# Node sums with features on partitions, node inputs made a group ahead, lead of 22

## The chip, the cores and the metric

The kernel runs on one NeuronCore of one Trainium2 chip. The metric is device time in microseconds (us). TensorE (PE), VectorE (DVE), ScalarE (ACT) and GpSimd (POOL) each work through their own queue of instructions in order; SyncE (SP) issues DMAs. An instruction waits on semaphores for those on other engines, and what stands behind it on its engine waits with it.

## The reference

One layer of a graph network with a normalisation ahead and a residual behind, N = 6250 nodes of D = 256 features, E = 206250 edges sorted by target node (33 a node on average), all in f32:

```python
h   = maximum(layernorm(x), 0)
e   = relu(raw @ W_e1.T + b_e1) @ W_e2.T + b_e2        # raw: 64 features an edge
emb = (e * (clip(polarity, 0, 1) + 0.01)) @ W_le.T + b_le
msg = relu(h[src] + emb)
agg = segment_sum(msg, dst, num_segments=N)
t   = (h + agg) @ W_g1.T + b_g1
out = x + relu(layernorm(t) * ln_g + ln_b) @ W_g2.T + b_g2
```

## The kernel before

**Start.** `nodes_out` computes h in chunks of 512 nodes, adds b_le and stores the sum as hb_d in DRAM (DVE's statistics, ACT's normalisation L324, POOL's addition L328, SP's store L329). The row statistics, 1/std and -mean/std of each node, remain in rs_s and nm_s, nodes on partitions. W_e2 and W_le are multiplied into one matrix wc_s, their biases into bc_s. Meanwhile the first LEAD = 20 units of edges go through their dense part.

**Edges.** A unit is 256 edges, two units make a block of 512, two blocks a pair, for which SP loads the raw features (L210, 256 KB, four buffers). There are 806 units. For each unit `edge_part` runs eight matmuls' records of L241 into PSUM (pz) and DVE adds bc_s (L246) into msg; on some of the first units ACT copies (L244) and DVE adds later (L502). Every fourth unit is a turn: the first layer of the pair after next (L223 on PE, L227 on ACT), then the sums that have become possible, then the next load. PSUM has seven buffers pz, shared by all of this.

POOL gathers the rows hb_d[src] by indirect DMA into hg (16 buffers, two gathers a unit). When they are there, `whole` computes relu(msg * polarity + hg): two DVE operations (L504) and one of ACT (L506). It follows `edge_part` at a distance of LEAD units, which falls by one every 36 units down to one.

**Sums.** A group is six blocks, 3072 edges of consecutive targets, in four strands of 32 rows each. `select` makes one-hot matrices (L494), and `add_up` adds the messages of a block into pd in PSUM (L514). After the last block of a group ACT copies pd to ms (L520): 128 rows of partial node sums.

**Nodes.** A window is 128 nodes (49 windows). Its sum comes from the two or three groups that may hold its edges: those within MARGIN = 1024 edges of the expected place, 146 pairs in all. When the last of them is done, `node_work` puts steps on a list by unit number; after each unit `due` runs one of those that have come due. The steps and their distance in units:

- `spread` (1 unit after the group's end): SP loads x (L183), DVE makes a one-hot matrix s for each group (L556);
- `rows_of` (2 later): PE multiplies the one-hots with ms (L565, the nodes on the partitions of the result), ACT computes h of the window from x (L567), DVE adds both into a (L568);
- `turned` (2 later): PE transposes a (L141), ACT copies the result to aT (L144);
- `one` (2 later): PE multiplies by W_g1 (L153), DVE adds the bias and normalises (L155 to L159);
- `two` (3 later): PE transposes (L165), ACT applies scale, offset and relu (L168);
- `three` (2 later): PE multiplies by W_g2 (L175), DVE adds bias and x (L177, L178), SP stores (L179).

The order of instructions on every engine is the order in which this program emits them. The function any_order, behind a condition at the end, is for edges in another order and isn't run with this input.

Of the kernel before, what the change touches and what calls it, by code (L numbers as in the profile page):

```python
# [12 lines left out]
ALU = mybir.AluOpType  # L13
# [24 lines left out]
MARGIN = 1024  # L38
DEG = E // N
LEAD = 20  # L40
# [4 lines left out]
CH = 4  # L45
assert DEG * N == E and NF * GE + S * P >= E
# [32 lines left out]

def rows(ap, t, p, n):  # L80
    return ap[t * P:t * P + p * n, :].rearrange("(t p) d -> p t d", p=p)
# [3 lines left out]
def gnn_kernel(ctx: ExitStack, tc: tile.TileContext, x, src_c, dst_c, dst_r, pol_c, raw_t, w_e1t, w_e2,  # L85
               w_let, w_g1t, w_g2t, vec_c, row_v, out):
# [4 lines left out]
    hb_d = dram.tile([N, D], F32, name="hb_d")  # L91

# [41 lines left out]
    def finish_nodes(nd, ps, w, n):  # L134
# [37 lines left out]
        def third(nT, xt):  # L172
# [6 lines left out]
            nc.sync.dma_start(out=out[bass.ds(r, n), :], in_=ot[:n])  # L179

        def load_x():
            xt = nd.tile([P, D], F32, name="xt3")
            nc.sync.dma_start(out=xt[:n], in_=x[bass.ds(r, n), :])  # L183
            return xt
# [6 lines left out]
    with fast:  # L191
# [20 lines left out]
        def first_layer(q):  # L212
# [12 lines left out]
            for c in range(2):  # L225
                for s, b in enumerate(bs):
                    nc.scalar.activation(e1[b][:, c, :], pe[s, c], AF.Relu, bias=be1_s[:, c:c + 1])  # L227
            raw.pop(q)

        def plain(u):  # L230

            return u < LEAD and u % 2 == 1
# [33 lines left out]
        nc.vector.memset(ones, 1.0)  # L266
        make_identity(nc, ident)
# [24 lines left out]
        with tc.tile_pool(name="p1", bufs=4) as p1, tc.tile_pool(name="p1x", bufs=6) as p1x:  # L292
# [4 lines left out]
            def load_rows(k, halves=1):  # L297
                if k < len(parts):
# [3 lines left out]
                    for i in range(halves):  # L302
                        nc.sync.dma_start(out=xts[k][:p, i * h:(i + 1) * h], in_=rows(x, t0 + i * h, p, h))
# [12 lines left out]
            def nodes_out(k):  # L316
# [12 lines left out]
                nc.sync.dma_start(out=rows(hb_d, t0, p, t), in_=hb[:p, :t])  # L329
# [30 lines left out]
            load_rows(4)  # L360
            load_pair(3)
            first_layer(0)
            lists = {3: (src_s, src_c), 5: (pol_s, pol_c), 7: (dst_f.bitcast(I32), dst_c)}
            for k in range(len(parts) + 1):
# [6 lines left out]
                if k:  # L371
                    nodes_out(k - 1)
                    load_rows(k + 4)
                    u = next(units, None)
                    if u is not None:
                        forward(u)
# [6 lines left out]
                if k % 2:  # L383
# [6 lines left out]
                if k == len(parts) - 3:  # L390
                    nc.vector.tensor_scalar(pol_s, pol_s, 0.0, 1.0, op0=ALU.max, op1=ALU.min)
                    nc.vector.tensor_scalar_add(pol_s, pol_s, 0.01)
            for u in units:
                forward(u)

# [16 lines left out]
        def rows_of_edges():  # L412
# [4 lines left out]
            nc.vector.tensor_tensor(rel[:, full:], dst_f[:, full:], base_b[:, NF, :], ALU.subtract)  # L417

# [42 lines left out]
        with tc.tile_pool(name="hg", bufs=HG) as hg_p, tc.tile_pool(name="ms", bufs=5) as ms_p, \  # L461
                tc.tile_pool(name="sel2", bufs=9) as sel2_p, tc.tile_pool(name="nd", bufs=2) as nd, tc.tile_pool(name="idx", bufs=HG) as idx_p:
# [45 lines left out]
            def add_up(b):  # L508
# [9 lines left out]
                if b == blocks_of(g)[-1]:  # L518
# [26 lines left out]
            def node_work(w, spread_now=False):  # L545
                n = min(P, N - w * P)
                gs = groups_of(w)
                box = {}
                turn, first, second, third, load_x = finish_nodes(nd, ps, w, n)

                def spread():
                    box["xt"] = load_x()
                    box["sel2"] = []
# [5 lines left out]
                    if not spread_now:  # L559
                        at(now + 2, rows_of)  # L560

                def rows_of():
                    pa = ps()
                    for i, g in enumerate(gs):
                        nc.tensor.matmul(pa[:n, 0, :], box["sel2"][i][:, :n], ms[g], start=i == 0, stop=i == len(gs) - 1)  # L565
# [233 lines left out]
```

## Time and profile before

| what | value |
|---|---|
| median of 10 runs | 2664.91 us (2655.61 to 2673.22) |
| the profiled execution | 2669.87 us, its span 2668.1 us |
| mean granted TensorE clock in it | 0.949 |
| PE busy in 0 to 20 us, and in the 28 us from 2640 on | 13.71 and 16.40 us |
| PE busy in 400 to 600 and 1400 to 1600 us | 183.42 and 173.84 us |
| first gather | 76.54 us |

The span runs from the first to the last instruction; the profiled execution's own time contains it. A group's line in the profile names line, engine, operation, tiles (out<-in) and count, then busy time and the mean duration of one in ns, and then the idle time of the engine just before these instructions and what ended it. A matmul in f32 appears as two records; records overlap, so the mean duration of one is longer than its share. The granted clock is the share of TensorE's full clock that was granted.

### The profile page before, as it was taken

The page shows a single profiled execution, that of the slowest core. Times are in us where ns is not written, and L with a number is a line of the kernel's source. Part 1 is how long each engine was busy: PE and PEld are TensorE (multiplying, and loading weights), DVE is VectorE, ACT ScalarE, POOL GpSimd, SP SyncE. Part 2 cuts the span into 40 slices and gives each one's busy share as a digit, 9 for nine tenths or more (in the row PEclk, how much of TensorE's full clock was granted, in tenths as well). Part 3 has the DMA queues.
Part 4 walks back from the last instruction along what each step waited for, and adds up shares of the span by engine and source line. Part 5 has one row for each costly group of instructions (what it writes and reads, how often), then busy time and mean ns, then how long its engine had stood idle before and what let it go on. Part 6 is the DMA issues. An engine that isn't in the chain of part 4 may idle for free.

```text
span 2668.1 us, 35462 instructions
## 1 busy us (share of the span) xinstructions
PE 2376.5 (89%) x12188; PEld 1643.3 (62%) x12188; DVE 1483.6 (56%) x3982; ACT 1115.7 (42%) x2003; POOL 1669.5 (63%) x1674
## 2 busy tenths in 40 slices
PE   8688989898999989899887988898899898988998
PEld 6456666566666656666665666665566666656665
DVE  5456555555565646555555565564466555556555
ACT  7234434344444434444433443443344443434343
POOL 5656656666666666666666666666666666666663
PEclk9889999999999989999998999999999999999999
DMA  7433333333333333333333333333334333333331
GB/s 268 122 103 107 105 115 109 103 114 113 104 115 102 114 109 114 109 100 113 113 107 99 109 110 110 100 110 101 114 105 118 106 101 112 110 103 106 110 108 54
DMA packets 135546, 296.34 MB, mean 111 GB/s; under 512 B 31256, under 2 KB 57408, under 8 KB 135360
## 3 DMA queue, kind: packets, MB, share of 16 engines
q0 software_dynamic: 77376, 211.39, 27.5%
q1 hardware_dynamic: 56848, 79.36, 9.4%
q10 hardware_dynamic: 1136, 3.27, 0.3%
q8 instruction: 97, 1.59, 0.3%
q14 instruction: 89, 0.73, 0.1%
HBM read 281.09 MB, written 12.80 MB: 110 GB/s over the span
## 4 chain that ended last, share of the span: by engine, by line
PE 78%; DVE 7%; issue 5%; another core or an unknown queue 5%; ACT 2%; DMA 1%; POOL 0%; SPq 0%; DVEq 0%; ACTq 0%; POOLq 0%
PE pz L241 48%; PE pz L223 13%; PE pd L514 8%; DVE hg L504 3%; PE pz L565 3%; PE pz L175 2%; PE pz L153 2%; DVE msg L246 2%; ACT hg L506 1%; PE pz L141 1%; DVE idx L474 1%; PE pz L165 0%; ACT aT L144 0%; DMA hg<-hb_d,idx 0%
## 5 line engine op out<-in xcount | busy, mean ns | idle before, releaser
L485 POOL DMA_INDIRECT hg<-hb_d,idx x1612 | 1633.0, 1013 | 934.4 <-DVE hg L504 431.9
L241 PE MATMUL pz<-wc_s,e 128*128 128x256 f32 x6448 | 1547.8, 393 | 45.5 <-issue 36.5
L241 PEld LDWEIGHTS pz<-wc_s,e 128*128 128x128 f32 x6448 | 1243.9, 196 | 307.4 <-issue 109.7
L246 DVE TENSOR_TENSOR msg<-pz,bc_s 128x512 f32<-128x512 f32 x796 | 545.8, 686 | 847.6 <-PE pz L241 345.7
L506 ACT ACTIVATE hg<-hg 128x512 f32<-128x512 f32 x806 | 507.4, 632 | 1204.3 <-DVE hg L504 1082.6
L504 DVE SCALAR_TENSOR_TENSOR hg<-msg,pol_s,hg 128x256 f32<-128x256 f32 x1612 | 703.0, 477 | 12.2 <-DMA hg<-hb_d,idx 11.7
L227 ACT ACTIVATE e<-pz,vecs 128x512 f32<-128x512 f32 x806 | 492.5, 685 | 168.9 <-PE pz L223 63.5
L223 PE MATMUL pz<-raw,we_s 64*128 64x512 f32 x1612 | 418.7, 621 | 18.2 <-DVE msg L246 8.2
L514 PE MATMUL pd<-hg,sel 128*32 128x256 f32 x3224 | 256.3, 390 | 56.1 <-issue 43.2
L223 PEld LDWEIGHTS pz<-raw,we_s 64*128 64x128 f32 x1612 | 144.7, 188 | 193.6 <-issue 163.7
L514 PEld LDWEIGHTS pd<-hg,sel 128*32 128x32 f32 x3224 | 92.4, 109 | 271.3 <-issue 214.0
L565 PE MATMUL pz<-ms,s 128*128 128x256 f32 (+1 forms) x292 | 92.5, 464 | 101.0 <-DVE s L556 86.3
L474 DVE COPY idx<-src_s 128x2 int32<-128x2 int32 x806 | 150.8, 190 | 0.0
L565 PEld LDWEIGHTS pz<-ms,s 128*128 128x128 f32 (+1 forms) x292 | 61.9, 224 | 123.8 <-issue 105.5
L177 DVE TENSOR_TENSOR ot<-pz,rows_b 128x256 f32<-128x256 f32 (+1 forms) x49 | 20.8, 424 | 196.2 <-PE pz L241 142.5
L153 PE MATMUL pz<-wg_s,aT 128*128 128x256 f32 (+1 forms) x196 | 57.1, 417 | 54.7 <-ACT aT L144 54.7
L520 ACT ACTIVATE ms<-pd 128x256 f32<-128x256 f32 x68 | 26.4, 388 | 133.4 <-PE pz L241 85.3
L153 PEld LDWEIGHTS pz<-wg_s,aT 128*128 128x128 f32 (+1 forms) x196 | 35.5, 197 | 73.1 <-ACT aT L144 69.5
L494 DVE TENSOR_TENSOR sel<-iota_w,rel 128x768 f32<-128x768 f32 x68 | 63.9, 940 | 0.0
L568 DVE TENSOR_TENSOR a<-a,pz 128x256 f32<-128x256 f32 (+1 forms) x49 | 20.7, 421 | 73.2 <-ACT a L567 41.1
L175 PE MATMUL pz<-wg_s,nT 128*128 128x256 f32 (+1 forms) x196 | 59.9, 432 | 1.0 <-DVE idx L474 0.7
L328 POOL TENSOR_TENSOR hb<-xt,rows_b 128x256 f32<-128x256 f32 (+1 forms) x49 | 34.9, 746 | 32.9 <-ACT xt L324 19.9
(73 smaller groups left out, 448.3 us busy)
## 6 DMA issues: line engine op xcount, KB each, us to landing
raw<-in_raw_t_dram SPq DMA_DIRECT2D x202, 256.0 KB
hg<-hb_d,idx POOLq DMA_INDIRECT x1612
hb_d<-hb SPq DMA_DIRECT2D x12, 512.0 KB
xt<-in_x_dram SPq DMA_DIRECT2D x48, 128.0 KB
out_dram<-ot SPq DMA_DIRECT2D x48, 128.0 KB
xt<-in_x_dram SPq DMA_DIRECT2D x11, 512.0 KB
src_s<-in_src_c_dram ACTq DMA_DIRECT2D x1, 806.0 KB
pol_s<-in_pol_c_dram ACTq DMA_DIRECT2D x1, 806.0 KB
```

Of the source, the lines that this page charges most:

```text
L153: nc.tensor.matmul(ph[:n, 0, :], aT[:, c, :n], wg1_s[:, c, :], start=c == 0, stop=c == 1)
L175: nc.tensor.matmul(po[:n, 0, :], nT[:, c, :n], wg2_s[:, c, :], start=c == 0, stop=c == 1)
L223: nc.tensor.matmul(pe[s, c], we1_s[s * F:(s + 1) * F, c * P:(c + 1) * P], raw[q][s * F:(s + 1) * F, :], start=True, stop=True)
L227: nc.scalar.activation(e1[b][:, c, :], pe[s, c], AF.Relu, bias=be1_s[:, c:c + 1])
L241: nc.tensor.matmul(pz[:, i, :], e1[b][:, c, k:k + P], wc_s[:, c, :], start=c == 0, stop=c == 1)
L246: nc.vector.tensor_add(msg[u], pz, bc_s)
L474: nc.vector.tensor_copy(idx[asked], src_s[:, 2 * asked:2 * asked + 2])
L485: nc.gpsimd.indirect_dma_start(out=hg[u][:, i, :], out_offset=None, in_=hb_d, in_offset=bass.IndirectOffsetOnAxis(ap=idx[u][:, i:i + 1], a ...
L504: nc.vector.scalar_tensor_tensor(hg[u][:, i, :], m[:, i, :], pol_s[:, 2 * u + i:2 * u + i + 1], hg[u][:, i, :], op0=ALU.mult, op1=ALU.add)
L506: nc.scalar.activation(hg[u], hg[u], AF.Relu)
L514: nc.tensor.matmul(pd[j * W:(j + 1) * W, g % 2, :], sel[g][:, k * S + j, :], m[:, j % 2, :], start=k == 0, stop=b == blocks_of(g)[-1])
L565: nc.tensor.matmul(pa[:n, 0, :], box["sel2"][i][:, :n], ms[g], start=i == 0, stop=i == len(gs) - 1)
```

## The change

The parts that the steps below touch:

- `rows_of` swaps its operands. ms is now the stationary one, in two halves of 128 features, and the one-hot the moving one, so the sum of a window comes out with features on partitions (two tiles of 128 x 128). `turned` goes, and with it L141, L144, and L567, L568. One DVE operation on PSUM adds the sum to relu of hT.
- hT is x of the window with features on partitions, from x_t, a transposed copy of x that is one more input. It is normalised by `ready`: two DVE operations with 1/std and -mean/std of the 128 nodes along the free axis, the same on all partitions. Those come from st_d in DRAM, which `stats_out` writes once (rs_s and nm_s transposed), by a load that repeats them over the partitions.
- `node_work` starts at the end of the group before the window's last: loads and one-hots 2 units after it, `ready` 3 units later. The sums come 2 units after the end of the last group. Then `one` 3, `two` 5, `three` 4 units apart (2, 3, 2 for the last windows). The buffers of node tiles go from 2 to 3.
- MARGIN is 768: 140 pairs of group and window. LEAD is 22.
- At the start x is loaded up to ten chunks ahead (11 buffers, 6 before), every third of the lead's units instead of every second is copied by ACT, one first-layer activation in four of the first blocks runs on DVE, the units stand in another rhythm, and the two operations on polarity come after the lead. The tail of 106 rows is moved in two DMAs of 96 and 10 rows.

```diff
-MARGIN = 1024
+MARGIN = 768
-LEAD = 20
+LEAD = 22
+AHEAD = 10
...
+def spread_out(p):
+
+    m = p - p % 16
+    return [(a, b) for a, b in ((0, m), (m, p)) if a < b]
...
-                    nc.scalar.activation(e1[b][:, c, :], pe[s, c], AF.Relu, bias=be1_s[:, c:c + 1])
+                    if b < 2 * LEAD // 4 + 4 and s == c == 1:
+                        nc.vector.tensor_scalar(e1[b][:, c, :], pe[s, c], be1_s[:, c:c + 1], 0.0, op0=ALU.add,
+                                                op1=ALU.max)
+                    else:
+                        nc.scalar.activation(e1[b][:, c, :], pe[s, c], AF.Relu, bias=be1_s[:, c:c + 1])
...
-            return u < LEAD and u % 2 == 1
+            return u < LEAD and u % 3 == 1
...
-                    load_rows(k + 4)
-                    u = next(units, None)
-                    if u is not None:
-                        forward(u)
+                    load_rows(k - 1 + AHEAD)
...
-                if k % 2:
+                for _ in range((k > 0) + (k > 2 and k % 3 > 0)):
...
-                if k == len(parts) - 3:
-                    nc.vector.tensor_scalar(pol_s, pol_s, 0.0, 1.0, op0=ALU.max, op1=ALU.min)
-                    nc.vector.tensor_scalar_add(pol_s, pol_s, 0.01)
             for u in units:
                 forward(u)
+            nc.vector.tensor_scalar(pol_s, pol_s, 0.0, 1.0, op0=ALU.max, op1=ALU.min)
+            nc.vector.tensor_scalar_add(pol_s, pol_s, 0.01)
...
+        def stats_out():
+
+            pt = ps()
+            for i, t in enumerate((rs_s, nm_s)):
+                nc.tensor.transpose(pt[:NW, i, :P], t, ident)
+            st_s = w0.tile([NW, 2, P], F32, name="st_s")
+            nc.scalar.activation(st_s, pt[:NW, :, :P], AF.Copy)
+            nc.sync.dma_start(out=st_d, in_=st_s)
...
                     for w in range(NW):
                         if groups_of(w)[-1] == g:
-                            late.pop(w, lambda: node_work(w))()
+                            late.pop(w)()
+                        elif groups_of(w)[-1] == g + 1 < NG - 1:
+                            late[w] = node_work(w)
...
+                far_apart = (3, 5, 4) if gs[-1] < NG - 3 else (2, 3, 2)
...
                 def spread():
                     box["xt"] = load_x()
+                    box["hT"] = nd.tile([P, 2, P], F32, name="hT")
+                    nc.sync.dma_start(out=box["hT"][:, :, :n], in_=x_t[:, :, w * P:w * P + n])
+                    st = nd.tile([P, 2, P], F32, name="stb")
+                    nc.sync.dma_start(out=st, in_=st_d[w:w + 1].to_broadcast([P, 2, P]))
+                    box["st"] = st
...
                     if not spread_now:
-                        at(now + 2, rows_of)
+                        at(now + 3, ready)
+
+                def ready():
+
+                    hT, st = box["hT"], box["st"]
+                    for i, op in enumerate((ALU.mult, ALU.add)):
+                        nc.vector.tensor_tensor(hT[:, :, :n], hT[:, :, :n], st[:, i:i + 1, :n].to_broadcast([P, 2, n]), op)

                 def rows_of():
+
+                    if spread_now:
+                        ready()
+                    hT = box["hT"]
                     pa = ps()
-                    for i, g in enumerate(gs):
-                        nc.tensor.matmul(pa[:n, 0, :], box["sel2"][i][:, :n], ms[g], start=i == 0, stop=i == len(gs) - 1)
-                    a = nd.tile([P, D], F32, name="a")
-                    nc.scalar.activation(a[:n], box["xt"][:n], AF.Relu, bias=nm_s[:n, w:w + 1], scale=rs_s[:n, w:w + 1])
-                    nc.vector.tensor_add(a[:n], a[:n], pa[:n, 0, :])
-                    box["a"] = a
-                    at(now + 2, turned)
-
-                def turned():
-                    box["aT"] = turn(box["a"])
-                    at(now + 2, one)
+                    for c in range(2):
+                        for i, g in enumerate(gs):
+                            nc.tensor.matmul(pa[:, c, :n], ms[g][:, c * P:(c + 1) * P], box["sel2"][i][:, :n],
+                                             start=i == 0, stop=i == len(gs) - 1)
+                    nc.vector.scalar_tensor_tensor(hT[:, :, :n], hT[:, :, :n], 0.0, pa[:, :, :n], op0=ALU.max, op1=ALU.add)
+                    at(now + far_apart[0], one)

                 def one():
-                    box["hs"] = first(box["aT"])
-                    at(now + 3, two)
+                    box["hs"] = first(box["hT"])
+                    at(now + far_apart[1], two)

                 def two():
                     box["nT"] = second(box["hs"])
-                    at(now + 2, three)
+                    at(now + far_apart[2], three)
...
                 if spread_now:
                     spread()
                 else:
-                    at(now + 1, spread)
-                return lambda: at(now + 1, rows_of)
+                    at(now + 2, spread)
+                return lambda: at(now + 1 + (gs[-1] < NG - 1), rows_of)
...
+        "x_t": laid(np.asarray(x).T.reshape(2, P, N).transpose(1, 0, 2)),
```

More of the change, by code (lines that the diff above doesn't have):

```diff
@@ L85, in gnn_kernel @@
 def gnn_kernel(ctx: ExitStack, tc: tile.TileContext, x, src_c, dst_c, dst_r, pol_c, raw_t, w_e1t, w_e2,
-               w_let, w_g1t, w_g2t, vec_c, row_v, out):
+               w_let, w_g1t, w_g2t, vec_c, row_v, x_t, out):
     nc = tc.nc
@@ L91, in gnn_kernel @@
     hb_d = dram.tile([N, D], F32, name="hb_d")
+    st_d = dram.tile([NW, 2, P], F32, name="st_d")
     def load(name, shape, src, eng):
@@ L178, in third @@
             nc.vector.tensor_add(ot[:n], ot[:n], xt[:n])
-            nc.sync.dma_start(out=out[bass.ds(r, n), :], in_=ot[:n])
+            for a, b in spread_out(n):
+                nc.sync.dma_start(out=out[bass.ds(r + a, b - a), :], in_=ot[a:b])
         def load_x():
             xt = nd.tile([P, D], F32, name="xt3")
-            nc.sync.dma_start(out=xt[:n], in_=x[bass.ds(r, n), :])
+            for a, b in spread_out(n):
+                nc.sync.dma_start(out=xt[a:b], in_=x[bass.ds(r + a, b - a), :])
             return xt
@@ L266, in gnn_kernel @@
         nc.vector.memset(ones, 1.0)
+        nc.vector.memset(rs_s, 0.0)
+        nc.vector.memset(nm_s, 0.0)
         make_identity(nc, ident)
@@ L289, in gnn_kernel @@
         be2_b = w0.tile([P, 2, P], F32, name="be2_b")
-        with tc.tile_pool(name="p1", bufs=4) as p1, tc.tile_pool(name="p1x", bufs=6) as p1x:
+        with tc.tile_pool(name="p1", bufs=4) as p1, tc.tile_pool(name="p1x", bufs=11) as p1x:
             parts = list(chunks())
@@ L302, in load_rows @@
                     for i in range(halves):
-                        nc.sync.dma_start(out=xts[k][:p, i * h:(i + 1) * h], in_=rows(x, t0 + i * h, p, h))
+                        for a, b in spread_out(p):
+                            nc.sync.dma_start(out=xts[k][a:b, i * h:(i + 1) * h], in_=rows(x, t0 + i * h, p, h)[a:b])
             def stats(k, i0, i1):
@@ L328, in nodes_out @@
                     nc.gpsimd.tensor_add(hb[:p, i, :], xt[:p, i, :], ble_b[:p])
-                nc.sync.dma_start(out=rows(hb_d, t0, p, t), in_=hb[:p, :t])
+                for a, b in spread_out(p):
+                    nc.sync.dma_start(out=rows(hb_d, t0, p, t)[a:b], in_=hb[a:b, :t])
             def product():
@@ L360, in gnn_kernel @@
             load_rows(4)
+            load_rows(5)
             load_pair(3)
+            for k in range(6, AHEAD):
+                load_rows(k)
             first_layer(0)
@@ L461, in gnn_kernel @@
         with tc.tile_pool(name="hg", bufs=HG) as hg_p, tc.tile_pool(name="ms", bufs=5) as ms_p, \
-                tc.tile_pool(name="sel2", bufs=9) as sel2_p, tc.tile_pool(name="nd", bufs=2) as nd, tc.tile_pool(name="idx", bufs=HG) as idx_p:
+                tc.tile_pool(name="sel2", bufs=9) as sel2_p, tc.tile_pool(name="nd", bufs=3) as nd, tc.tile_pool(name="idx", bufs=HG) as idx_p:
             idx = {}
@@ L604, in gnn_kernel @@
             for i, fn in enumerate((first_rows, rows_of_edges, lambda: select(0), lambda: select(1), row_numbers,
-                                    node_weights)):
+                                    node_weights, stats_out)):
                 at(LEAD + i, fn)
```

## The prediction

> **What bounds the kernel now.** I read the page's busy shares and its slices first, then the groups with the idle time before them, the table of waits, and last the timeline around a node step, with the granted clock of that stretch.
>
> The page of the kernel before (its span and engine rows, two groups of matmuls of the node work, the matmul group of the edges; a group's last part is the idle time of the engine just before it and what ended it):
>
> ```profile
> span 2668.1 us, 35462 instructions
> PE 2376.5 (89%) x12188; PEld 1643.3 (62%) x12188; DVE 1483.6 (56%) x3982; ACT 1115.7 (42%) x2003; POOL 1669.5 (63%) x1674
> ...
> L241 PE MATMUL pz<-wc_s,e 128*128 128x256 f32 x6448 | 1547.8, 393 | 45.5 <-issue 36.5
> ...
> L565 PE MATMUL pz<-ms,s 128*128 128x256 f32 (+1 forms) x292 | 92.5, 464 | 101.0 <-DVE s L556 86.3
> ...
> L153 PE MATMUL pz<-wg_s,aT 128*128 128x256 f32 (+1 forms) x196 | 57.1, 417 | 54.7 <-ACT aT L144 54.7
> ```
>
> TensorE is busy for 2376.5 of 2668.1 us and no other engine passes 63%, so PE bounds the kernel, and only its own work, its idle time (291.6 us) and its clock can change the time. Two rows of node work hold more than half of that idle time: 101.0 us before L565 and 54.7 us before L153, together 155.7 us, although they are only 150 us of PE's busy time. L241, with ten times the busy time, waits 45.5 us. In the table of waits (waiting engine and line, what ended the wait, sum, times, longest):
>
> ```profile
> DVE msg L246 <- PE pz L241: 345.7, 156, 7.5
> PE pz L565 <- DVE s L556: 86.3, 27, 8.7
> ACT ms L520 <- PE pz L241: 85.3, 29, 5.5
> PE pz L153 <- ACT aT L144: 54.7, 37, 3.8
> ```
>
> VectorE runs behind PE: its msg addition waits 7.5 us at worst for the signal of a matmul. By matching each L246 with the last L241 of its unit I get a lag of about 2.2 us in the middle and about 6 to 8 us in one unit of twenty. The one-hot tiles (L556) stand in that same queue only two units (2 x 1.73 us of PE) ahead of the matmuls that need them, so they come late. A timeline row shows it (start, duration, engine, line; in brackets the idle time before):
>
> ```profile
> 339.10 0.67 DVE L556 TENSOR_SCALAR s<-iota_p,rowid 128x128 f32<-128x128 f32 x3
> ...
> 339.50 1.54 PEld L565 LDWEIGHTS pz<-ms,s 128*128 128x128 f32 x6 [3.04 <-issue]
> 339.53 2.24 PE L565 MATMUL pz<-ms,s 128*128 128x256 f32 x6 [2.67 <-DVE s L556]
> ...
> 341.56 2.92 PE L241 MATMUL pz<-wc_s,e 128*128 128x256 f32 x8
> ```
>
> PE stood still for 2.67 us, ms (L520) had been written 4.46 us earlier, and only the one-hots were missing. It also pays afterwards: six L565 records take 2.24 us and eight L241 take 2.92, where after a wait of 1.32 us, at 300.58, the same groups took 1.53 and 1.89. The granted clock was 0.66 in the 5 us after the long wait and 1.00 after the short one. One long wait therefore costs another 0.71 + 1.03 = 1.74 us.
>
> **The change part by part**, against the profiled execution's 2669.9 us (span 2668.1).
>
> *One-hots a group ahead.* All that L565 waited for was L556. Issued with the loads about 12 units earlier, it is no longer late. What is late next is ms: its copy on ScalarE ends 4.7 us on average after the group's last L514 matmuls (1.9 us in the quickest tenth, 6.9 in the slowest). Against that, the order of instructions puts the new sums only two units after those matmuls in 28 windows (0.4 + 3.46 = 3.9 us of PE) and three units in some 18; before it was three in all. Moving each old wait to that distance, with ms where the trace has it, leaves 0.32 us a window at three units and 0.76 at two: 18 x 0.32 + 28 x 0.76 = 27, about 28 us with the last two windows. So -73 us. Ends: -101 (no ms wait) and -27 (the delays of all 68 copies against 3.9 us give 1.55 us, taken for 48 windows).
>
> *The transposition and its step go.* L153 waited for aT through PE, ACT and PE again, two units apart. Now the result of the sums is already turned, DVE's one instruction after them feeds L153, and a first layer and an L514 burst (1.9 + 1.0 us) mostly lie between: 3 x 1.73 + 2.9 = 8.1 us of cover against a lag that passes 6 to 8 us in a twentieth of units. I leave 5 us: -50 us. Ends: -55, -25.
>
> *Clock.* 27 of the 70 waits at these two rows are followed by a stretch at half clock (counted from the clock's rows). 27 x 1.74 = 47 us; in proportion to the waits that go (123 of 156), -37 us. The Trainium skill, "TensorE: Matmul & The Clock Gate", section "Why this matters for your kernels", warns of PE-idle gaps over about 3 us; with the window of its Part 1, 3.4 us, only 12 waits (8 + 4) would count, 12 x 1.74 = 21 us, or -16 in proportion. The row above shows a wait of 2.67 us followed by the slow clock, so the trace decides; 16 and 47 are the ends.
>
> *PE's work.* 98 transpositions of 128 columns go. Two of them take 0.38 us in the timeline where one lasts 0.275: spaced 0.105, so -10 us. The sums were 292 records of 256 columns at a spacing of (1.53 - 0.38) / 5 = 0.22 us, about 63 us. Now 140 pairs of group and window (6 fewer, by the smaller margin) make 560 records of 128 columns, each with its own weight load. A rule speaks against this: the same page, Part 3, section "The mechanism", says that weight loads overlap running matmuls only when they go to other row groups. Load and matmul would then follow each other: 0.105 + 0.105 each, 118 us, +55. But L241 keeps a spacing of 0.216 with a 128-column load in every record, 1243.9 us of loads inside 1547.8 of matmuls, and the 128-column transpositions load theirs too at 0.105. By these rows 560 x 0.105 = 59 us. I take the rows: -12 us altogether; ends -15 and +45.
>
> *VectorE and ScalarE.* Per window DVE loses one addition (0.42) and gets two products over SBUF (row L178, 0.43 each) and one operation on PSUM (0.48 by L504): +0.92 x 49 = 45 us. ACT loses L567 and L144, 0.95 x 49 = 46 us. Neither bounds (56 and 42%), but a node wait of PE is also the time in which DVE catches up. PE's waits put down to DVE or ACT at L241, L223 and L514 are now about 23 us (3.1 + 2.9 + 8.2 + 5.4 + 3.7). I double them and add a quarter of the new DVE work: +35 us. Ends 0 and +80 (half of what the two steps lose).
>
> *Loads.* Each window gets two more transfers of 128 KB: 12.5 MB on 296, with DMA at 30 to 40% busy. SP queues them with the output stores (which it holds for L178, 1085.8 us in all) and the edge loads behind. Edge loads have about two turns of four units in hand, some 20 us, so this costs nothing; without that cover, their issue (0.4 us each) would be 2 x 0.4 x 49 = 39 us. The new DVE wait for them (hT times st) stands three units after the issue; queued behind it are the msg additions and the hg products, for which ScalarE, then PE, wait. The x loads of the loop needed 1.0 to 4.0 us by the packets of ten of them, under the 5.2 us of cover: nothing.
>
> *Start.* Loading rows further ahead, a lead of 22, one activation in four moved to DVE and another rhythm of units shift work inside the first 76 us, after which gathers start (the first at 76.54, when the last hb rows land). Splitting the 106-row tail into 96 + 10 may land it sooner. -3 us with the shorter end; ends -8 and +6. Two units more of lead cost nothing in the loop: the gathers, 2.5 us a unit, (0.95 and 0.30 between, twice), are quicker than PE's 3.3 (2668 / 806).
>
> Sum: -73 - 50 - 37 - 12 + 35 - 3 = -140 us, so 2530 for the profiled execution. The median of the runs (2664.9) lies 5 us under it: **2525 us**.
>
> **Rivals.**
> 1. *ms takes the one-hots' place* (2590 us). For it: ACT already waits 85.3 us for PE at L520, and the sums move one unit closer. Then L565 keeps about 70 us and its clock loss: -31 - 50 - 25 - 12 + 45 - 3 = -76. Against it: ms was 2 to 7 us early at nearly all long waits.
> 2. *More goes* (2460 us). DVE's lag shrinks with PE's stalls: waits -101 and -55, clock -47, work -15, start -3, replaced waits +15: -206. For it: L246's 847.6 us of idle time show a DVE that waits more than it works late. Against it: the lag comes from signals of PE that this change does not touch.
> 3. *The waits only move* (2640 us): DVE still lags and PE stalls at L223 and L241, when PSUM buffers run out. Of 156 + 47 us only 25 are kept. Against it: DVE idles 44%.
> 4. *Slower* (2700 us): the DVE wait for hT and st. If they land 9 us or more after their issue, DVE stands for 4 us a window with everything behind it; PE has some 2 units in hand at best, and what remains over 2.9 us (140 / 49) a window turns the gain into a loss. 4 us makes -140 + 4 x 49 = +56, less some 20 of the slack: +36. The longest x load seen, 4.0 us, speaks against it; 512-byte rows are not in the trace.
> That the change does nothing is no rival: the order of instructions shows the sums, one-hots and loads moved.
>
> **Chances.** The forecast's own case (2490 to 2565) 0.45, rival 1 0.22, rival 2 0.15, rival 3 0.10, rival 4 0.08. The range 2450 to 2630 leaves out the far side of 2, part of 3, and 4. Within 0.2% (5 us, what runs of this kernel can tell) only the edge of 3 falls: 0.03. Slower takes 4 and a little of 3: 0.10. Faster: 0.87.
>
> **What would show it.** In the changed profile the row of the new sums should wait some 30 us, for ACT's ms and not DVE's one-hots; the L153 row under 10 us; the mean clock near 0.965 instead of 0.949; matmuls of the sums spaced 0.1 us (a spacing of 0.2 proves the rule on weight loads); DVE waiting for no hT landing. Wrong would be: a wait of 60 us or more at the sums (rival 1), PE idle time grown at L241, L223 and L514 by over 80 us (3), or DVE idle before the hT products (4).

## The result and the profile after

| | before | changed |
|---|---|---|
| median of the runs | 2662.09 us (2649.39 to 2674.0, 31 runs) | 2621.99 us (2616.29 to 2628.39, 9 runs) |
| profiled execution, its span | 2669.87, 2668.1 us | 2633.04, 2631.3 us |
| mean granted TensorE clock | 0.949 | 0.949 |

The ratio is 0.9849 [0.9828, 0.9870]: the changed kernel is faster by 40 us, where 140 were forecast. The range held the time; the forecast's own case (2490 to 2565) did not.

These jobs, and two later ones, ran in a **held** condition, in which the kernel before takes 2618 to 2665 us, and four other jobs in a **quiet** one, in which it takes 2239 to 2241. Ratios are taken within one job; where profiles of different jobs are compared, the text says so.

The page of the changed kernel (span and engine rows, then groups of matmuls: the edges L255, the first layer L233, the strands L540, the new sums L611, the first node multiplication L161):

```profile
span 2631.3 us, 35590 instructions
PE 2410.0 (92%) x12360; PEld 1654.0 (63%) x12360; DVE 1516.1 (58%) x4083; ACT 1061.9 (40%) x1895; POOL 1670.5 (63%) x1674
...
L255 PE MATMUL pz<-wc_s,e 128*128 128x256 f32 x6448 | 1562.7, 393 | 79.6 <-issue 74.4
...
L233 PE MATMUL pz<-raw,we_s 64*128 64x512 f32 x1612 | 465.8, 636 | 52.7 <-issue 33.2
L540 PE MATMUL pd<-hg,sel 128*32 128x256 f32 x3224 | 271.7, 410 | 59.5 <-issue 41.8
...
L611 PE MATMUL pz<-s,ms 128*128 128x128 f32 (+1 forms) x560 | 81.6, 292 | 16.8 <-issue 11.1
...
L161 PE MATMUL pz<-wg_s,hT 128*128 128x256 f32 (+1 forms) x196 | 52.3, 389 | 0.6 <-issue 0.6
```

The first layer's row of the kernel before:

```profile
L223 PE MATMUL pz<-raw,we_s 64*128 64x512 f32 x1612 | 418.7, 621 | 18.2 <-DVE msg L246 8.2
```

The two waits are gone, and more thoroughly than forecast: 101.0 + 54.7 us before, 16.8 + 0.6 now, so 138.3 us less. But the idle time before the edges' matmuls rose from 45.5 to 79.6 (+34.1) and before the first layer from 18.2 to 52.7 (+34.5), and PE is busy for 33.5 us more (2376.5 to 2410.0), though it has less to do. -138.3 + 68.6 + 33.5 - 0.6 (all other rows) = -36.8 us, the difference of the spans. So the time was saved where the prediction put it, and taken back elsewhere.

Where, the table of waits of the same profile says (engine and line, what ended the wait, sum, times, longest):

```profile
PE pz L255 <- issue: 74.4, 110, 2.2
...
PE pz L233 <- issue: 33.2, 34, 4.4
...
PE pz L255 <- DVE msg L260: 2.1, 5, 1.1
```

"issue" means that PE waited for nothing that the profile shows. In all, such idle time of PE rose from 93.6 us in 125 pieces to 162.3 in 222. VectorE's release of PSUM buffers ends 2.1 us at L255. Rows of the timeline show such a place:

```profile
96.26 0.19 PEld L255 LDWEIGHTS pz<-wc_s,e 128*128 128x128 f32 x1 [1.71 <-issue]
96.46 0.95 POOL L511 DMA_INDIRECT hg<-hb_d,idx  x1 [0.30 <-issue]
...
97.71 0.94 POOL L511 DMA_INDIRECT hg<-hb_d,idx  x1 [0.30 <-issue]
97.91 0.38 PE L255 MATMUL pz<-wc_s,e 128*128 128x256 f32 x1 [2.01 <-issue]
...
99.33 0.29 PEld L255 LDWEIGHTS pz<-wc_s,e 128*128 128x128 f32 x1 [2.88 <-issue]
100.03 0.59 PE L255 MATMUL pz<-wc_s,e 128*128 128x256 f32 x1 [1.74 <-issue]
```

Weight load, matmul, weight load, matmul: one instruction each 0.7 or 1.4 us, of the same unit and with all their inputs there, while GpSimd issues a gather each 1.25 us as ever. I call it a **slow stretch** and count one where three or more such starts in a row lie over 0.54 us apart with no semaphore waited for. What it costs is the excess over 0.1 us a start. This count is a rough one. It hangs on how nearly coincident starts are joined, and it takes in matmuls of 512 columns at half clock, which start 0.84 to 0.86 us apart (experiment 4 comes to that); the one stretch of each quiet profile is first-layer matmuls of 512 columns in the first 10 us, 0.81 us apart. So two stricter measures stand beside it. One is PE's idle time that "issue" ended. The other is **late starts**: loads and matmuls that the program makes wait for nothing, and that start 0.70 or 1.40 us (within 0.03) after the load or matmul before. A lost semaphore record cannot make a late start, since these instructions wait for no semaphore.

| profile | slow stretches | lost in them, us | idle ended by "issue", us | late starts | semaphore records of PE, DVE and ACT in the trace |
|---|---|---|---|---|---|
| before, first job | 23 | 113 | 93.6 | 114 | 6729 of 8801 |
| changed, first job | 47 | 216 | 162.3 | 186 | 6346 of 8468 |
| before, quiet job | 1 | 3 | 0 | 1 | 8795 of 8801 |
| changed, quiet job | 1 | 3 | 0 | 0 | 8461 of 8468 |

By the first count the changed kernel lost some 100 us more in slow stretches than the one before; all measures rise by half or more. The table of windows compares one stretch of time in the first job and in a quiet one (window, length, then busy time and instructions of PE, PEld, DVE, ACT and POOL, the granted clock, the DMA share, GB/s); the changed kernel, first job:

```profile
94.00:122.00 28.00, 12.02 (x29) 5.16 (x31) 5.05 (x12) 2.44 (x5) 17.02 (x18) 0.58 0.41 122
1000.00:1028.00 28.00, 25.92 (x132) 18.26 (x131) 16.13 (x44) 11.34 (x21) 18.59 (x20) 0.94 0.46 136
```

and in a quiet job:

```profile
94.00:122.00 28.00, 26.82 (x151) 17.48 (x151) 19.86 (x48) 11.49 (x20) 21.60 (x22) 1.00 0.53 156
1000.00:1028.00 28.00, 28.00 (x161) 19.46 (x160) 19.70 (x52) 14.35 (x25) 21.45 (x22) 1.00 0.50 147
```

29 matmuls against 151 in the same 28 us of the same program; elsewhere 132 against 161.

### The profile page after: what moved, and what is told of

Its sections match the earlier page's. It is cut to its first block, busy times and chain, and to the rows that moved or that the text cites. A ratio compares the mean times of both kernels' runs of the same rounds, so it can differ in the third digit from the quotient of the medians.

```text
span 2631.3 us, 35590 instructions
## 1 busy us (share of the span) xinstructions
PE 2410.0 (92%) x12360; PEld 1654.0 (63%) x12360; DVE 1516.1 (58%) x4083; ACT 1061.9 (40%) x1895; POOL 1670.5 (63%) x1674
## 4 chain that ended last, share of the span: by engine, by line
PE 85%; issue 7%; DVE 4%; another core or an unknown queue 2%; ACT 1%; DMA 1%; SPq 0%; POOL 0%; DVEq 0%; ACTq 0%
PE pz L255 55%; PE pz L233 15%; PE pd L540 9%; PE pz L611 3%; PE pz L183 2%; PE pz L161 2%; DVE hg L530 2%; DVE msg L260 1%; ACT e L241 1%; PE pz L173 0%; DVE idx L500 0%; ACT hg L532 0%; DMA raw<-in_raw_t_dram 0%; DMA hg<-hb_d,idx 0%
## 5 line engine op out<-in xcount | busy, mean ns | idle before, releaser
L255 PE MATMUL pz<-wc_s,e 128*128 128x256 f32 x6448 | 1562.7, 393 | 79.6 <-issue 74.4
L255 PEld LDWEIGHTS pz<-wc_s,e 128*128 128x128 f32 x6448 | 1233.0, 196 | 377.8 <-issue 149.5
L241 ACT ACTIVATE e<-pz,vecs 128x512 f32<-128x512 f32 x799 | 486.4, 685 | 140.2 <-remote 49.0
L233 PE MATMUL pz<-raw,we_s 64*128 64x512 f32 x1612 | 465.8, 636 | 52.7 <-issue 33.2
L540 PE MATMUL pd<-hg,sel 128*32 128x256 f32 x3224 | 271.7, 410 | 59.5 <-issue 41.8
L233 PEld LDWEIGHTS pz<-raw,we_s 64*128 64x128 f32 x1612 | 159.4, 190 | 247.8 <-issue 187.3
L540 PEld LDWEIGHTS pd<-hg,sel 128*32 128x32 f32 x3224 | 96.9, 113 | 289.3 <-issue 235.3
L611 PE MATMUL pz<-s,ms 128*128 128x128 f32 (+1 forms) x560 | 81.6, 292 | 16.8 <-issue 11.1
L611 PEld LDWEIGHTS pz<-s,ms 128*128 128x128 f32 x560 | 76.9, 203 | 24.4 <-issue 14.8
L613 DVE SCALAR_TENSOR_TENSOR hT<-hT,pz 128x256 f32<-128x256 f32 (+1 forms) x49 | 20.4, 416 | 81.8 <-remote 24.2
L161 PE MATMUL pz<-wg_s,hT 128*128 128x256 f32 (+1 forms) x196 | 52.3, 389 | 0.6 <-issue 0.6
L161 PEld LDWEIGHTS pz<-wg_s,hT 128*128 128x128 f32 (+1 forms) x196 | 38.7, 198 | 7.4 <-issue 1.1
L183 PEld LDWEIGHTS pz<-wg_s,nT 128*128 128x128 f32 (+1 forms) x196 | 37.6, 193 | 8.1 <-issue 2.5
```

The source lines that it names most:

```text
L161: nc.tensor.matmul(ph[:n, 0, :], aT[:, c, :n], wg1_s[:, c, :], start=c == 0, stop=c == 1)
L183: nc.tensor.matmul(po[:n, 0, :], nT[:, c, :n], wg2_s[:, c, :], start=c == 0, stop=c == 1)
L233: nc.tensor.matmul(pe[s, c], we1_s[s * F:(s + 1) * F, c * P:(c + 1) * P], raw[q][s * F:(s + 1) * F, :], start=True, stop=True)
L255: nc.tensor.matmul(pz[:, i, :], e1[b][:, c, k:k + P], wc_s[:, c, :], start=c == 0, stop=c == 1)
L540: nc.tensor.matmul(pd[j * W:(j + 1) * W, g % 2, :], sel[g][:, k * S + j, :], m[:, j % 2, :], start=k == 0, stop=b == blocks_of(g)[-1])
L611: nc.tensor.matmul(pa[:, c, :n], ms[g][:, c * P:(c + 1) * P], box["sel2"][i][:, :n], start=i == 0, stop=i == len(gs) - 1)
```

## Experiments

**1. The parts alone (quiet job, before 2239.32 us).** My first theories were A (the stretches follow PE's number of instructions), B (the new loads cause them) and C (dense work of PE causes them). Four kernels: the changed one with its one-hots made after the group's end again;

```diff
+                    if spread_now:
+                        hots()
+                    else:
+                        at(now + 3, ready)
+
+                def hots():
...
-                        at(now + 3, ready)
+                        at(now + 2, rows_of)
...
-                return lambda: at(now + 1 + (gs[-1] < NG - 1), rows_of)
+                return lambda: at(now + 1, rows_of if spread_now else hots)
```

> The changed kernel with its one-hots made late again, one unit after the end of a window's last group and two units before the sums, as in the kernel before; all else as changed. The waits of the kernel before at the sums come back (17 us now, about 100 then). Theory A (PE cannot be supplied with instructions or drain their records at full rate for long: after some 30 us without a pause it falls into a stretch of one instruction each 0.7 us, so a wait pays for itself): the waits return but the slow stretches get fewer, from 47 to about 30, and the time rises by 0 to 45 us. Rival B (the loads or their packets cause the slow stretches): they stay at 47 and the time rises by 83 us of waits and some 20 us of clock, about 100 us in all, to 2720.

the changed one without the window loads (every window takes hT and st of the first);

```diff
-                    nc.sync.dma_start(out=box["hT"][:, :, :n], in_=x_t[:, :, w * P:w * P + n])
-                    st = nd.tile([P, 2, P], F32, name="stb")
-                    nc.sync.dma_start(out=st, in_=st_d[w:w + 1].to_broadcast([P, 2, P]))
-                    box["st"] = st
+                    box["st"] = st_one
...
```

> The changed kernel with hT and st loaded once instead of for each window, so every window takes the numbers of the first; 98 transfers of 128 KB and some 20,000 packets go. Theory A: slow stretches stay at about 47, time within 15 us of the changed kernel's 2622. Rival B (loads or their packets cause them): the stretches fall to the 23 of the kernel before and the time to about 2530.

the one before with one-hots and loads a group ahead;

```diff
-                            late.pop(w, lambda: node_work(w))()
+                            late.pop(w)()
+                        elif groups_of(w)[-1] == g + 1 < NG - 1:
+                            late[w] = node_work(w)
...
-                    if not spread_now:
-                        at(now + 2, rows_of)
...
-                    at(now + 1, spread)
-                return lambda: at(now + 1, rows_of)
+                    at(now + 2, spread)
+                return lambda: at(now + (1 if spread_now else 3), rows_of)
```

> The kernel before with one part of the change alone: x and the one-hots of a window are made a group ahead, the sums stay three units after the group's end; no loads, no other operands, no other distances. The wait at the sums (101 us) falls to about 15. Theory A: the slow stretches grow from 23 to about 33 and eat over half of it, the time falls by 15 to 45 us. Rival B: no new transfers, so no new slow stretches; the time falls by the 86 us of waits and some 25 us of clock, to about 2550.

and the changed one with the edge part in records of 512 columns.

```diff
-            for i in range(2):
-                k = (2 * v + i) * P
-                for c in range(2):
-                    nc.tensor.matmul(pz[:, i, :], e1[b][:, c, k:k + P], wc_s[:, c, :], start=c == 0, stop=c == 1)
+            k = 2 * v * P
+            for c in range(2):
+                nc.tensor.matmul(pz, e1[b][:, c, k:k + P], wc_s, start=c == 0, stop=c == 1)
```

> The changed kernel with the edge matmuls of a unit as two of 512 columns instead of four of 256: the same columns through PE with half the instructions of that group (6448 fewer matmul and load records each becomes 3224); it multiplies another part of e, so the messages are others. Theory A (instruction or record rate): the slow stretches nearly vanish, at most 10 are left, and the time falls by 120 to 220 us. Rival C (the stretches come from PE being dense, whatever its instructions): they stay at 40 to 55 and the time stays within 30 us.

Measured: 2217.24 us (ratio 0.9902 [0.9886, 0.9919]), 2217.79 (0.9902), 2239.54 (0.9998 [0.9989, 1.0008]) and 2211.31 (0.9876 [0.9859, 0.9892]). All expectations in microseconds missed, because there were no slow stretches to change. What the runs do say: in a quiet job neither early one-hots nor the loads are worth anything, and the rest of the change gives 1%.

**2. Both kernels, the start and the wide records (quiet job, before 2240.40 us).**

> The changed kernel once more. Where TensorE is busy for 99% of the span in the kernel before (a chip like that of the first four runs, before at 2239 us): all theories say 2217 us, ratio 0.990, and the gain is 12 us in the start and 9 us in TensorE's own work; its L611 row waits for nothing (under 3 us). Where TensorE falls into stretches of one instruction per 0.70 us (before at 2660 us): Theory A (these stretches follow TensorE's rate of instructions, and take back what the waits gave) says ratio 0.985, again with more than 40 such stretches against some 23 in the kernel before; the rival (they came by chance in one execution) says a different count, and a ratio of 0.95 to 0.97.

> The kernel before once more, for its profile on the same chip as the others. On a chip like that of the first four runs: L565 and L153 wait under 5 us together (both theories), so that the 141 us of waits belong to the chip of the first profile, not to the order of the program. Rival: they wait 100 us or more and the time is lower for another reason.

The third kernel is the changed one with the old start:

```diff
-LEAD = 22
+LEAD = 20
...
-            return u < LEAD and u % 3 == 1
+            return u < LEAD and u % 2 == 1
...
-        with tc.tile_pool(name="p1", bufs=4) as p1, tc.tile_pool(name="p1x", bufs=11) as p1x:
+        with tc.tile_pool(name="p1", bufs=4) as p1, tc.tile_pool(name="p1x", bufs=6) as p1x:
...
-                for _ in range((k > 0) + (k > 2 and k % 3 > 0)):
+                for _ in range(k % 2):
...
```

> The changed kernel with the start of the one before (lead of 20, six buffers for x, the old rhythm of units, no split of the tail). If the start is worth 12 us, as the time of unit 22 says: 2229 us on the quiet chip, ratio 0.9955 against before. If it is worth 3 us, as the prediction had it: 2220 us, ratio 0.991. On a chip with slow stretches: ratio 0.990 and 0.986.

The fourth is the kernel before with the same edit as wide.

> The kernel before with the edge part of a unit as two records of 512 columns instead of four of 256 (the same columns streamed, half the matmul and weight-load instructions; it multiplies another part of e, so its messages are others). On the quiet chip all say -6 us, ratio 0.997, as the changed kernel gained 6 us by the same edit. On a chip with slow stretches: Theory A (stretches cost by the instruction) says 60 us or more less, ratio below 0.975; Theory C (stretches come from dense streaming, cost by the time) says within 20 us.

Measured: 2220.06 us (0.9912 [0.9895, 0.9928]), 2239.54, 2228.67 (0.9948 [0.9931, 0.9965]) and 2231.61 (0.9964 [0.9950, 0.9979]). The page of the kernel before in this job, span, engines and the rows shown earlier:

```profile
span 2237.8 us, 35462 instructions
...
PE 2204.8 (99%) x12188; PEld 1584.2 (71%) x12188; DVE 1504.0 (67%) x3982; ACT 1110.1 (50%) x2003; POOL 1629.1 (73%) x1674
...
L565 PE MATMUL pz<-ms,s 128*128 128x256 f32 (+1 forms) x292 | 71.0, 380 | 0.3 <-DVE s L556 0.3
...
L153 PE MATMUL pz<-wg_s,aT 128*128 128x256 f32 (+1 forms) x196 | 50.2, 380 | 0.0
```

and of the changed one:

```profile
span 2216.6 us, 35590 instructions
...
PE 2190.4 (99%) x12360; PEld 1582.5 (71%) x12360; DVE 1533.6 (69%) x4083; ACT 1064.2 (48%) x1895; POOL 1649.8 (74%) x1674
...
L611 PE MATMUL pz<-s,ms 128*128 128x128 f32 (+1 forms) x560 | 70.8, 275 | 0.5 <-ACT ms L546 0.5
```

The same program in the same order waits 0.3 us at the two steps instead of 155.7. So the waits on which the forecast stood were not a property of the order of the program. PE works 99% of the time, and the change can only give what it takes off PE's work and off the start: unit 22's matmuls start 12.3 us earlier (78.7 to 66.4), the loop to unit 800 is 8.0 us shorter, the end 0.9. Putting the old start back costs 8.6 us.

**3. A lag put in by hand (two quiet jobs, before 2239.51 and 2240.49 us).** In the first profile VectorE began the msg addition 2.05 us after the unit's last matmul in the median, in 12% of units over 5 us; in the quiet profile 0.04 us, and 1.6%. If that lag made the waits, extra work on VectorE must bring them back:

```diff
...
+            if u % 10 == 5 and u > 40:
+                for _ in range(8):
+                    nc.vector.tensor_add(lag_s, bc_s, bc_s)
```

> The kernel before with eight extra additions on VectorE (about 5.5 us together, into a tile that nobody reads) ahead of the msg addition of every tenth unit after unit 40, so that VectorE lags behind TensorE as it did in the first profile, on a chip where it otherwise doesn't. If the waits of the two node steps were the work of that lag (Theory D), they come back: L565 for DVE's one-hots and L153 together 30 us or more, and the time rises by 30 to 120 us over before. If they were something of the first chip alone (rival E), they stay under 10 us and the time rises by less than 15 us.

> The changed kernel with the same extra additions. Theory D with the prediction's mechanism: the sums (L611) and the first multiplication (L161) wait under 10 us together, and the changed kernel with the lag beats the one before with the lag by what these two steps lose there, on top of the 20 us that it gains without a lag. Rival F (the waits only move): TensorE waits as long elsewhere, at L233, L255 and L540, and the distance between the two stays at 20 us.

Measured: 2333.19 us (1.0417 [1.0399, 1.0434]) and 2291.50 (1.0226 [1.0209, 1.0243]). The two rows of the kernel before with the lag:

```profile
L569 PE MATMUL pz<-ms,s 128*128 128x256 f32 (+1 forms) x292 | 74.2, 392 | 5.1 <-DVE s L560 5.1
...
L153 PE MATMUL pz<-wg_s,aT 128*128 128x256 f32 (+1 forms) x196 | 52.3, 391 | 15.7 <-ACT aT L144 15.7
```

and of the changed one:

```profile
L615 PE MATMUL pz<-s,ms 128*128 128x128 f32 (+1 forms) x560 | 74.4, 281 | 6.2 <-ACT ms L550 6.2
...
L161 PE MATMUL pz<-wg_s,hT 128*128 128x256 f32 (+1 forms) x196 | 50.1, 379 | 0.0
```

The waits came back, though at 20.8 us and not 30 or more; and the distance between the kernels grew from 20 to 41.7 us. Rival F falls: most of the extra 21 us is what the two steps lose with the lag, 15.7 + 5.1 of idle time, less the 6.2 that the sums now wait for ms, and some 2 us in longer records (5.3 us more busy at L569 and L153 than in experiment 2, 3.3 at L615 and L161). Most of the lag's price (71 of 94 us) stays in the changed kernel, 31 of it at the first layer (L234 busy for 435.0 us, 403.9 without the lag). But the lag put in was of the first profile's kind (1.42 us in the median against 2.05, over 5 us in 18% of units against 12%), and it brought back 20.8 of 155.7 us. That the rest of those waits came from VectorE's lag is not shown. Which part of the change earns the 21 us, two more kernels say, the edits of experiment 1 with the lag added:

> The kernel before with the extra additions on VectorE, and its one-hots and loads made a group ahead: the one-hot part of the change alone, under the lag. The kernel before with the lag took 2333.2 us on a chip where before took 2239.5; its L569 row lost 9.7 us (4.8 of idle time and 4.9 in longer records), L153 20.8. If the rows price it: 4 to 10 us less than with the lag alone (ratio to before 1.037 to 1.040), L569 now waiting for ms. By the prediction's shares (73 of 123 us for the one-hots) it would be 13 us or more less (ratio under 1.036).

> The changed kernel with the extra additions, but its one-hots made after the group's end, as before the change: all of the change but the early one-hots, under the lag. The changed kernel with the lag took 2291.5 us, ratio 1.0226. If the transposition step is what the change gains by under a lag: 2292 to 2298 us, ratio 1.023 to 1.026. By the prediction's shares: 2304 us or more, ratio over 1.028, and the sums wait for VectorE's one-hots by 10 us or more.

Measured: 2325.25 us (1.0381 [1.0363, 1.0398]) and 2295.21 (1.0246 [1.0229, 1.0263]). Early one-hots alone give 8 us, and taking them away from the changed kernel costs about 4.5 (0.0020 of 2240, less than the intervals can tell from nothing). The rest, 13 to 17, is left for the vanished transposition step by subtraction, with whatever else the lag changes; with early one-hots alone L153 still waits 17.5 us. The prediction's shares (73 to 50) are the other way round here. That L569 would then wait for ms was wrong: it waits 0.0.

**4. What brings the slow stretches on (held job, before 2623.34 us).** Since traces with slow stretches lack a quarter of their semaphore records, recording itself was suspect (Theory G).

```diff
...
+            if u > 40:
+                for _ in range(4):
+                    nc.scalar.activation(fl_s, bc_s[:, 0, 0:1], AF.Copy)
+                nc.sync.dma_start(out=fl_d[u % 4], in_=bc_s[:, 0, 0:64])
```

> The kernel before with four tiny copies on ScalarE and a store of 128 packets of 256 bytes in every unit after unit 40 (3060 more instructions on ScalarE, 765 more DMAs, some 98,000 more packets). If stretches of one TensorE instruction per 0.70 us come when there is more for the trace to record (Theory G), they appear here: ten or more of them, semaphore records missing, 50 us or more longer than before. If they belong to a chip's state (rival H): none, all records there, and the time within 10 us of before, since ScalarE is busy for 50% and DMA for 45%.

The other two kernels are before_wide and the changed one again.

> As before_wide (it multiplies another part of e). Where before takes 2240 us: ratio 0.996 again, nothing new. Where it takes 2660 us: below 0.975 if the stretches cost by the instruction, within 20 us if they come from dense streaming.

> The changed kernel. Where before takes 2240 us: 0.991. Where it takes 2660 us: 0.985, with more than 40 slow stretches if they follow from how densely TensorE is fed, another number if they came by chance.

Measured: flood 2644.06 us (1.0090 [1.0064, 1.0116]), 20 stretches, 94 us; before_wide_2 2575.47 (0.9828 [0.9763, 0.9893]), 33 stretches, 146 us; after_2 2588.21 (0.9877 [0.9814, 0.9939]), 43 stretches, 187 us. So the changed kernel has twice as many as flood in the same job, and its gain, 35 us, is again what it was: no chance of one execution. More records of ScalarE and of DMA did not bring more stretches (20; the kernel before had 23 in the first job, and no profile of it in this one was kept), so G is not supported for these. Theory B falls too: flood moves 110,000 more packets than the kernel before (245,734 against 135,546), where the change adds 20,500. flood's 21 us more fit neither theory's number.

Half the instructions in the edge part gained 48 us, against 9 in the quiet job. The 33 stretches say nothing here, since the rough count takes 512-column matmuls at half clock for slow, and these are the edge part's own here: 87 starts of before_wide_2 lie 0.84 to 0.86 us behind the one before, nearly all where half clock was granted; flood has 2 such starts. The stricter measures do. First the rows of flood, then those of before_wide_2:

```profile
L243 PE MATMUL pz<-wc_s,e 128*128 128x256 f32 x6448 | 1528.8, 390 | 47.1 <-issue 38.7
...
L520 PE MATMUL pd<-hg,sel 128*32 128x256 f32 x3224 | 264.5, 394 | 55.6 <-issue 43.0
```

```profile
L240 PE MATMUL pz<-wc_s,e 128*128 128x512 f32 x3224 | 1525.9, 615 | 47.9 <-issue 30.6
...
L513 PE MATMUL pd<-hg,sel 128*32 128x256 f32 x3224 | 226.1, 388 | 19.7 <-issue 10.9
```

| profile, this job | idle ended by "issue", us | late starts |
|---|---|---|
| flood | 96.0 | 127 |
| before_wide_2 | 48.1 | 57 |
| changed, again | 155.6 | 189 |

With three quarters of PE's instructions (8964 matmuls for 12188) and the same columns to stream, late starts and the idle time that "issue" ended fell to half. So the slow starts go with PE's instructions, as Theory A had it, though A's own mark (a ratio below 0.975) was missed; Theory C, by which dense streaming alone brings them, falls with its 20 us. Whether the supply of instructions or the draining of PE's own records is what holds PE up, no run here tells apart.

The same profiles warn of the forecast's base: the wait before L153 was 54.7 us in the first job, 19.2 in flood and 88.0 in before_wide_2, with the same node steps in all three.

The four profiles of before, changed and flood in this condition hold a pattern. I took the time since PE last stood idle for over 0.3 us (or since the last stretch ended), and how often a stretch began:

| time since the last pause | spent there, us | stretches begun | per 100 us |
|---|---|---|---|
| 0 to 10 us | 3771 | 15 | 0.4 |
| 10 to 20 us | 2650 | 28 | 1.1 |
| 20 to 30 us | 1521 | 23 | 1.5 |
| over 30 us | 1223 | 63 | 5.2 |

That is Theory I: a stretch comes after a long run without a pause, and the change took pauses away. In a recount by late starts, the first row comes out at 0.7 to 0.9 per 100 us and the last at 4.1 to 5.2, and 206 and 231 us of before and flood lie over 30 us behind the last pause, 343 and 477 of the two profiles of the changed kernel. It holds in the held condition alone: in the quiet jobs PE runs without such pauses for 99% of the span and starts nothing late.

**5. Pauses put in (held job, before 2618.44 us).** The changed kernel, with a one-element matmul every six units that waits for VectorE:

```diff
...
+            if u % 6 == 1 and u > 48:
+                nc.tensor.matmul(pz[:1, 0, :1], tick_s, tick_s, start=True, stop=True)
...
+            if u % 6 == 0 and u > 47:
+                nc.vector.tensor_copy(tick_s, pz[:, 1, 0:1])
```

> The changed kernel with a short pause of TensorE every six units (some 20 us): a one-element matmul ahead of the unit's edge part waits for a one-element copy on VectorE of the unit before it; 126 pauses. Where before takes 2240 us: each costs 0.4 to 1 us, 2270 to 2350 us, ratio 1.01 to 1.05. Where before takes 2620 to 2660 us, Theory I (a stretch of one instruction per 0.70 us comes after some 30 us without a pause): fewer than 20 stretches against 43 and 47 in the two profiles of the changed kernel, under 90 us lost in them against 187 and 216, and a time that the pauses' own 2 us or so each (250 us) may raise. Rival J (pauses don't matter, stretches come by chance or by a clock of their own): 35 or more stretches.

Measured: 2673.84 us (1.0216 [1.0170, 1.0262]), 16 stretches, 62 us lost. Its page:

```profile
span 2673.2 us, 36405 instructions
...
PE 2351.7 (88%) x12614; PEld 1652.5 (62%) x12614; DVE 1536.6 (57%) x4210; ACT 1075.1 (40%) x1895; POOL 1641.3 (61%) x1674
...
L254 PE MATMUL pz<-tick_s 128*1 128x1 f32 x254 | 24.0, 163 | 255.3 <-DVE tick_s L261 211.0
```

16 stretches against 43 and 47 bear Theory I out, and rival J falls; by the stricter measures, 49 late starts against 186 and 189. The changed kernel itself was not run in this job, so these are counts of three jobs. PE's busy time is 24 us below that of after_2 (2375.3), although it does more. VectorE's lag shrank too, from 2.1 and 2.5 us in the median to 0.36. But the pauses themselves cost 255.3 us, 2.0 each, and spared 125 to 154 us in stretches: a ratio of 1.0216 to before, where the changed kernel had 0.985 and 0.988. No version that beats both kernels came out of this.

## Why the prediction was wrong

**The step that failed** is the paragraph "VectorE and ScalarE", with its +35 us (0 to +80) for waits that take the place of the removed ones, and with it the clock's -37. The +35 counted only PE's waits for other engines at L241, L223 and L514. What took the removed waits' place has no such releaser: slow stretches, some 100 us more by my count, or 117 by the rows (68.6 of idle time, and 33.5 more busy where the quiet jobs show 14.4 less). Set against the forecast's sum: the two waits fell by 138.3 us (123 forecast), idle time elsewhere rose by 68 (35 forecast), and PE's busy time, which clock and work were to shorten by 49, rose by 33.5.

The kind was in view: the L241 row that I quoted says "45.5 <-issue 36.5", and I passed over it. Rival 3 came nearest (2640 against 2622) and named the right lines, L223 and L241, but not the cause: VectorE's release of PSUM buffers at msg ended 2.1 and 6.8 us of it. Its sign, idle time grown by over 80 us at L241, L223 and L514, came out at 72.

Term by term, forecast against measured:

- *One-hots*, -73: the row fell by 84 in the first job. Without a lag the term is 0 (0.9998), with the lag of experiment 3 it is 4 to 8 us.
- *Transposition step*, -50: the row fell by 54 in the first job; 0 in a quiet one; 13 to 17 with the lag.
- *Clock*, -37: the granted clock stayed 0.949. Stretches let it fall as waits did (0.58 in the window at 94 us); half clock was granted for 275 us before and 269 after.
- *PE's work*, -12: 14.4 us less busy in quiet jobs, nearly right by luck. The transpositions, put at 10, were 18.7 us; the sums, which were to shrink from 63 to 59, took 71.0 and 70.8. (The spacing worked out for them is 0.23, not 0.22, and -10 and -4 make -14.) The rule that was weighed there, weight loads in turn with matmuls (the Trainium skill, "TensorE: Matmul & The Clock Gate", Part 3, "The mechanism"), would have made the sums 118 us; L611 is 70.8 us for 560 records, 0.126 each, nearer to the rows' 0.105 than to 0.21.
- *Loads*, 0: right; without them 0.9902, with them 0.9912 in another job.
- *Start*, -3 (-8 to +6): mis-sized, 8.6 us by old_start and 12.3 by the time of unit 22. The first gather alone came 8.4 us sooner (75.99 to 67.56 us in the quiet profiles), where I had allowed 3.

The sum -73 - 50 - 37 was worked out from one trace as if its lag were a property of the kernel. The mechanism was right as far as it went: the changed kernel hardly waits at these two steps, in the first job and with a lag put in. That the time thus freed is PE's to use was wrong. The range held the time only because it took in a part of rival 3, which had the cause wrong; that is luck. Why the chip is held in some jobs is open, and so is what in flood moved the time.

## What to carry to other kernels

Before pricing a wait, look at what the bounding engine does between its waits: rows whose idle time ends with "issue", single instructions at an even distance, and missing semaphore records say that the trace holds something that is not in the program. Waits taken out of an engine that is 90% busy may come back as such time, so a saving counts only after asking what the engine's own pace is. And a second profile from another job is the cheapest check on a forecast built on waits: here the 155.7 us became 0.3.

## What the runs showed of the hardware

- The same program takes 2240 or 2618 to 2665 us by the job, on the same chip too (2240.5, and 2623.3 seven minutes later). In the slower condition VectorE's msg addition starts some 2 us later after its matmul in the median (2.05 against 0.04), TensorE falls into stretches of one instruction per 0.70 us, and the clock of the profiles is 0.949 to 0.955 against 0.992 to 0.999.
- In the slower condition a stretch is six to thirteen times as likely after 30 us without a pause as within 10 us of one (4.1 to 5.2 against 0.4 to 0.9 per 100 us), and a pause every 20 us cut the stretches from 43 and 47 to 16.
- With a quarter fewer TensorE instructions for the same columns, late starts fell from 127 to 57 in one job.
- In the traces of the slower condition 24% to 35% of the engines' semaphore records are missing, against 0.1% in the quiet ones. The Trainium skill, "NOTIFIC — the notification-queue block", section 7.1, says that a full queue of records either loses records or stalls the engine that produces them. The first is what these traces look like; that PE is stalled for it is not shown. flood, with 35% more such events, had no more stretches, but its events are ScalarE's, so records of TensorE's own are not ruled out.
